# Quantised x of a fused attention and LoRA kernel: transposed by DMA in place of TensorE

## The chip, the cores and the metric

The kernel runs on one core of one Trainium2 chip. The metric is the device time of one execution in microseconds; a comparison uses the median of several runs on the same chip. A core has a TensorE (matrix multiplications, results into PSUM), a VectorE, a ScalarE, a GpSimd ("POOL") and a SyncE ("SP"), each of which runs its own list of instructions in order. SP and ScalarE also issue the DMAs here, each into a queue of its own.

## What is computed

Two steps, for x of shape (2, 1024, 2048):

```python
q1 = fake_quant(layernorm(x), x1_scale, x1_zp)      # 8-bit grid, round and clip
q2 = fake_quant(ctx, x2_scale, x2_zp)
x  = x + q1 @ q2                                    # (1024 x 2048) @ (2048 x 2048) per batch
z  = layernorm(x)
x  = x + z @ kernel + bias + LoRA terms of z        # gated and shared A, B of rank 32
```

The quantised values minus 128 are whole numbers that bf16 holds exactly, so the first product runs in bf16; the second runs in float32.

## The kernel before

Both batches are done one after the other. Tokens are taken in tiles of 128 (`m`, 8 per batch), two tiles make a group `g` (4 per batch), columns of the output go in blocks `n` of 512.

**First product.** ctx arrives in pieces of 128 x 1024 float32 (512 KB) in ten buffers `lit`, loaded by SP ahead of need (`load_next`, L176). `quantise` turns a piece into int16 on ScalarE (L314), into three buffers `q2b`, and into bf16 on VectorE (L317). `prep_x` does the same for a token tile of x: `bn_stats` on VectorE (L283), the mean and root (L257 to L290, with a square root on ScalarE, L261), quantisation to 8 bits on ScalarE (L295), and then, for each half `h` of the 2048 columns, a conversion to bf16 on ScalarE that also sums the row (L298). Both the 8-bit and the bf16 form lie in one work buffer `wk`: `q8` has a place for each of two tiles in turn, `qh` has one place, which each tile overwrites. The product needs x with its 2048 columns on the partitions, so each half of `qh` is transposed: eight 128 x 128 blocks on TensorE against the bf16 identity `ident_h` into the PSUM tile `pt` (L303), and one copy on VectorE from there into `c1T[g]` (L304).

`xattn_pair(b, n, g)` multiplies a group by a column block: per token tile ScalarE writes a correction term into the PSUM tile `pa` (L359), 16 bf16 matmuls of 128 x 512 add to it (L361), and VectorE scales it and adds it to y (L370). `column_term` supplies the correction from ctx (L333, L345, L348).

**Where prep_x stands.** In batch 0: tiles 0 and 1 while the first ctx column block is quantised, tiles 2 and 3 between the first two pairs, tiles 4 to 7 among the later pairs. In batch 1: tiles 0 to 3 inside the last outer step of batch 0's second product (in `meanwhile`), tiles 4 to 7 as in batch 0.

**Second product.** `ffn` multiplies z by the weights with a two-level scheme of seven by seven block products (`product`, L611), with float32 operands that VectorE and POOL combine (L551, L560) and z that is transposed by TensorE (`prep_z`, L432, in float32, against `ident`) and copied by ScalarE (L433). Results are added to y on VectorE (L629) and stored by ScalarE's queue (L631).

**What sets the order.** A scheduling layer places the instructions of each engine, sets the semaphores for every dependence, and gives each DMA of SP and ScalarE one of eight completion semaphores (`DMAHW0` to `DMAHW7`) in turn. A DMA waits until the DMA before it on the same semaphore has landed, whichever queue issued that one. Within an engine and a queue the order is fixed: an instruction that waits holds up everything behind it.

Of the kernel before, what the change touches and what calls it, by code (L numbers as in the profile page):

```python
# [11 lines left out]
BF16 = mybir.dt.bfloat16  # L12
# [8 lines left out]
P = 128  # L21
# [45 lines left out]
def tile_quant_xattn_then_lora_ffn(  # L67
# [17 lines left out]
    nc = tc.nc  # L85
# [12 lines left out]
    H = D // 2  # L98
    KH = KT // 2
# [3 lines left out]
    const = ctx.enter_context(tc.tile_pool(name="const", bufs=1))  # L103
# [4 lines left out]
    ps_m = ctx.enter_context(tc.tile_pool(name="ps_m", bufs=2, space=PSUM))  # L108
# [27 lines left out]
    def bf(t, n):  # L136

        return t.rearrange("p k n -> p (k n)").bitcast(BF16).rearrange("p (k n) -> p k n", n=n)

    def flat(t):  # L140
        return t.rearrange("p k n -> p (k n)")
# [74 lines left out]

    ident = const.tile([P, P], F32, tag="ident", name="ident")
    make_identity(nc, ident)
    ident_h = const.tile([P, P], BF16, tag="ident_h", name="ident_h")
    nc.gpsimd.tensor_copy(ident_h, ident)  # L220
    ones_h = const.tile([P, P], BF16, tag="ones_h", name="ones_h")
    nc.gpsimd.memset(ones_h, 1.0)

# [5 lines left out]
    for tag in ("acc0", "acc1", "delta"):  # L229
# [11 lines left out]
        out=gate_b.rearrange("p b n -> p (b n)"),  # L241
        in_=gate.rearrange("b n -> (b n)").partition_broadcast(P),
# [11 lines left out]
    def norm_stats(stats, name):  # L254

        mv = small.tile([P, 2], F32, tag="mv", name=f"mv_{name}")
        nc.vector.bn_aggr(mv, stats.rearrange("p n s -> p (n s)"))  # L257
        ve = small.tile([P, 1], F32, tag="ve", name=f"ve_{name}")
        nc.vector.tensor_scalar_add(ve, mv[:, 1:2], EPS)
        sd = small.tile([P, 1], F32, tag="sd", name=f"sd_{name}")  # L260
        nc.scalar.activation(sd, ve, AF.Sqrt)  # L261
        r0 = small.tile([P, 1], F32, tag="r0", name=f"r0_{name}")
        nc.vector.reciprocal(r0, sd)

        t = small.tile([P, 1], F32, tag="nt", name=f"nt_{name}")
        nc.vector.scalar_tensor_tensor(t, ve, r0, r0, ALU.mult, ALU.mult)
        nc.vector.tensor_scalar(t, t, -0.5, 1.5, ALU.mult, ALU.add)
        rstd = small.tile([P, 1], F32, tag="rstd", name=f"rstd_{name}")
        nc.vector.tensor_mul(rstd, r0, t)
        return mv[:, 0:1], rstd  # L270
# [6 lines left out]
    def prep_x(b, m, c1T, wk):  # L277

        nm = f"{b}_{m}"
        g, tok = m // MG, ds((m % MG) * P, P)  # L280
        ym = y[g][:, m % MG, :]
        for n in range(NN):
            nc.vector.bn_stats(st1[:, m, n, :], ym[:, ds(n * NB, NB)])  # L283
        mean, rstd = norm_stats(st1[:, m], f"a{nm}")

        k = small.tile([P, 1], F32, tag="kx", name=f"kx_{nm}")
        nc.vector.tensor_mul(k, rstd, inv1)
        o = small.tile([P, 1], F32, tag="ox", name=f"ox_{nm}")
        nc.vector.tensor_mul(o, mean, k)
        nc.vector.tensor_sub(o, z1, o)  # L290

        wf = flat(wk)
        q8 = wf[:, ds((m % 2) * (D // 4), D // 4)].bitcast(U8)
        qh = wf[:, D // 2 : D].bitcast(BF16)
        nc.scalar.activation(q8, ym, AF.Identity, bias=o, scale=k)  # L295
        rsum = small.tile([P, 2], F32, tag="rsum", name=f"rsum_{nm}")
        for h in range(2):
            nc.scalar.activation(  # L298
                qh[:, ds(h * H, H)], q8[:, ds(h * H, H)], AF.Identity, bias=n_centre, accum_out=rsum[:, h : h + 1]
            )  # L300
            pt = ps_m.tile([P, KH, P], BF16, tag="pm", name=f"pt_{nm}_{h}")
            for kt in range(KH):
                nc.tensor.transpose(pt[:, kt, :], qh[:, ds(h * H + kt * P, P)], ident_h)  # L303
            nc.vector.tensor_copy(c1T[g][:, ds(h * KH, KH), tok], pt)  # L304

        r_c = small.tile([P, 1], F32, tag="r_c", name=f"r_c_{nm}")
        nc.vector.tensor_add(r_c, rsum[:, 0:1], rsum[:, 1:2])
        nc.vector.tensor_mul(r_s[:, m : m + 1], r_c, d2)
# [372 lines left out]
    c1T = [bf(t, GT) for t in c1T_bufs]  # L681
# [11 lines left out]
    for b in range(B):  # L693
# [6 lines left out]
        if b == 0:  # L700
            open_c2(0)
            prep_x(0, 0, c1T, wk)
            for r in range(NR):
                quantise(c2[0], r)
                if r == 3:
                    prep_x(0, 1, c1T, wk)
            for m in range(4, MT):
                load_x(0, m)
            open_c2(1)
            column_term(b, 0, c2[0])  # L710
        opened = xattn_pair(b, 0, 0, c1T, c2[0])
        if b == 0:
            for r in range(4):
                quantise(c2[1], r)
            for m in (2, 3):
                prep_x(b, m, c1T, wk)
# [138 lines left out]
        if b + 1 < B:  # L855
            c1T_bufs, c1T, wk = state["c1b"], state["c1T"], state["wk"]
# [53 lines left out]
```

## Time and profile before

| what | value |
|---|---|
| time, median of 3 runs | 1130.41 us (1127.37 to 1130.59) |
| profiled execution, its own time | 1128.61 us |
| its span in the trace | 1126.8 us, granted clock 0.999 |
| TensorE busy | 1072.4 us, 95%, 3926 matmuls |
| VectorE busy | 741.5 us, 66% |
| ScalarE busy | 261.1 us, 23% |
| POOL busy | 266.6 us, 24% |
| SP's DMA queue (q1) | 218.65 MB, 56.6% of 16 engines |
| ScalarE's DMA queue (q10) | 42.02 MB, 10.5% of 16 engines |

The profile page is one execution, recorded by the hardware profiler. Its first part gives each engine's busy time; the second cuts the span into 40 equal slices and gives for each the busy share in tenths; the fourth follows the chain of work that ended last back from the end; the fifth lists groups of instructions by source line (L303 is line 303 of the kernel), with their count, busy time and mean duration, and the idle time of the engine just before them with what ended it. Further views of the trace list the instructions in order of time, the busy time in chosen windows, and the instructions of one tile or one line with their waits. A share of busy time is an average over stages that are limited by different things, so the windows say more than the page's totals.

### The profile page before, as it was taken

Reading aid. Unit: us, or ns where it says so; the run is one execution under the profiler, and the core shown is the slowest. Engines: PE = TensorE matmul, PEld = TensorE weight load, DVE = VectorE, ACT = ScalarE, POOL = GpSimd, SP = SyncE. Lnnn points to the kernel's source line nnn. Section 1 sums busy time; section 2 is a strip of 40 time slices with the busy share of each in tenths; the row PEclk is TensorE's granted clock in tenths of the full one; section 3 lists DMA queues with packets and bytes.
Section 4 is the critical chain, followed back from the end, with each engine's and each line's share of the span. In section 5 each row is a group of like instructions: output and inputs, shape, how many; then the busy total and the mean of one; then the engine's idle time right before and its main releaser. Section 6 shows DMA issues by size and latency. Waiting matters only on the chain.

```text
span 1126.8 us, 10619 instructions
## 1 busy us (share of the span) xinstructions
PE 1072.4 (95%) x3926; PEld 489.3 (43%) x3926; DVE 741.5 (66%) x969; ACT 261.1 (23%) x342; POOL 266.6 (24%) x106
## 2 busy tenths in 40 slices
PE   1689899999999999999999999999999999999998
PEld 0244334554444444444444433455444444444443
DVE  4685547576696768568777654766668586865861
ACT  5875513320001010001375761232000000000000
POOL 0000000234253422525000000022535343243600
PEclk9999999999999999999999999999999999999999
DMA  8991935885789757489857094588668875749611
GB/s 307 391 244 35 282 124 217 298 322 205 246 285 377 266 181 264 141 301 355 285 184 228 1 277 154 182 301 314 244 215 293 295 255 181 256 145 322 213 38 56
DMA packets 120772, 261.35 MB, mean 232 GB/s; under 512 B 11920, under 2 KB 16144, under 8 KB 119568
## 3 DMA queue, kind: packets, MB, share of 16 engines
q1 hardware_dynamic: 99264, 218.65, 56.6%
q10 hardware_dynamic: 21456, 42.02, 10.5%
q8 instruction: 31, 0.51, 0.2%
q14 instruction: 21, 0.17, 0.0%
HBM read 224.99 MB, written 37.75 MB: 233 GB/s over the span
## 4 chain that ended last, share of the span: by engine, by line
PE 80%; DMA 7%; DVE 6%; ACT 4%; issue 1%; SPq 1%; ACTq 0%; DVEq 0%
PE fu L611 33%; PE fv L611 17%; PE pa L361 13%; PE fw L611 9%; DMA lit<-in_ctx_dram 4%; PE pl L483 3%; PE ptz L432 2%; DVE big L560 1%; PE pg_a L383 1%; DVE st L283 1%; PE pg_b L383 1%; ACT big L298 1%; ACT big L295 1%; DMA bd<-q2b 1%; DMA big<-in_w_dram 1%
## 5 line engine op out<-in xcount | busy, mean ns | idle before, releaser
L611 PE MATMUL fu<-big,lit 128*128 128x512 f32 x896 | 396.3, 594 | 2.4 <-DVE y L629 2.4
L560 POOL TENSOR_TENSOR lit<-lit,lit 128x1024 f32<-128x1024 f32 x56 | 165.2, 2957 | 539.4 <-PE pa L361 209.1
L611 PEld LDWEIGHTS fu<-big,lit 128*128 128x128 f32 x896 | 167.8, 190 | 208.2 <-issue 206.7
L361 PE MATMUL pa<-big,big 128*128 128x512 bf16 x1024 | 238.0, 382 | 11.9 <-ACT pa L359 10.6
L611 PE MATMUL fv<-big,lit 128*128 128x512 f32 x448 | 198.1, 594 | 0.0
L551 POOL TENSOR_TENSOR lit<-lit,lit 128x1024 f32<-128x1024 f32 x40 | 100.9, 2524 | 283.4 <-DMA lit<-zs 255.5
L560 DVE TENSOR_TENSOR big<-big,big 128x2048 f32<-128x2048 f32 x56 | 159.4, 2850 | 5.9 <-PE ptz L432 5.3
L361 PEld LDWEIGHTS <-big 128*128 128x128 bf16 x1024 | 97.0, 98 | 146.5 <-issue 44.3
L629 DVE TENSOR_TENSOR y<-y,fu 128x1024 f32<-128x1024 f32 (+1 forms) x98 | 113.7, 1194 | 67.2 <-PE fu L611 66.8
L611 PEld LDWEIGHTS fv<-big,lit 128*128 128x128 f32 x448 | 84.3, 190 | 105.0 <-issue 105.0
L629 DVE TENSOR_TENSOR y<-y,fv 128x1024 f32<-128x1024 f32 x48 | 56.8, 1218 | 91.1 <-PE fv L611 91.1
L478 ACT COPY pl<-bias 128x1024 f32<-128x1024 f32 x32 | 32.6, 1017 | 344.9 <-DVE y L493 327.1
L314 ACT ACTIVATE q2b<-lit,sc,inv 128x1024 int16<-128x1024 f32 x64 | 76.6, 1230 | 146.4 <-DMA lit<-in_ctx_dram 124.7
L551 DVE TENSOR_TENSOR big<-big,big 128x2048 f32<-128x2048 f32 x40 | 101.7, 2544 | 13.2 <-DMA big<-in_w_dram 13.2
L611 PE MATMUL fw<-big,lit 128*128 128x512 f32 x224 | 100.6, 596 | 0.1
L370 DVE SCALAR_TENSOR_TENSOR y<-pa,k_s,y 128x1024 f32<-128x1024 f32 x32 | 41.0, 1282 | 69.7 <-PE pa L361 69.7
L359 ACT ACTIVATE pa<-bp,r_s 128x512 f32<-128x512 f32 x64 | 42.8, 684 | 105.6 <-PE pa L361 60.5
L629 DVE TENSOR_TENSOR y<-y,fw 128x1024 f32<-128x1024 f32 x24 | 28.4, 1217 | 52.5 <-PE fw L611 52.5
L611 PEld LDWEIGHTS fw<-big,lit 128*128 128x128 f32 x224 | 41.3, 190 | 48.7 <-issue 48.2
L303 PE MATMUL pt<-ident_h,big 128*128 128x128 bf16 x256 | 20.3, 231 | 29.6 <-ACT big L298 29.4
L283 DVE BATCH_NORM_STATS2 st<-y 128x6 f32<-128x512 f32 x64 | 42.1, 680 | 2.9 <-DMA y<-in_x_dram 2.9
L317 DVE TENSOR_SCALAR big<-q2b 128x1024 bf16<-128x1024 int16 x64 | 27.6, 440 | 23.7 <-ACT q2b L314 20.5
(79 smaller groups left out, 609.9 us busy)
## 6 DMA issues: line engine op xcount, KB each, us to landing
big<-in_w_dram SPq DMA_DIRECT2D x96, 1024.0 KB
lit<-zs SPq DMA_DIRECT2D x88, 512.0 KB
lit<-in_ctx_dram SPq DMA_DIRECT2D x64, 512.0 KB
out_dram<-y ACTq DMA_DIRECT2D x30, 512.0 KB
zs<-lit ACTq DMA_DIRECT2D x24, 512.0 KB
y<-in_x_dram SPq DMA_DIRECT2D x8, 1024.0 KB
lit<-in_lora_a_dram SPq DMA_DIRECT2D x32, 256.0 KB
lit<-in_lora_bt_dram SPq DMA_DIRECT2D x32, 256.0 KB
```

Source lines behind the costliest of these rows:

```text
L283: nc.vector.bn_stats(st1[:, m, n, :], ym[:, ds(n * NB, NB)])
L314: nc.scalar.activation(qi, t, AF.Relu, bias=z2, scale=inv2)
L317: nc.vector.tensor_scalar(c2[r // 4][:, ds(2 * (r % 4), 2), :], qi, QMAX, CENTRE, ALU.min, ALU.subtract)
L359: nc.scalar.activation(pa[:, j, :], colt[n], AF.Identity, bias=r_s[:, m : m + 1])
L361: nc.tensor.matmul(pa[:, j, :], c1T[g][:, k, ds(j * P, P)], c2[k // 8][:, k % 8, :], start=False, stop=(k == KT - 1), skip_group_check=True,)
L370: summed = nc.vector.scalar_tensor_tensor(yp, pa, s12, yp, ALU.mult, ALU.add)
L478: nc.scalar.copy(pl, self.bb.unsqueeze(1).to_broadcast([P, 2, NB]))
L483: nc.tensor.matmul(pl[:, i, ds(h * (NB // 2), NB // 2)], axT[rows, pr, ds(j * P, P)], self.bp[rows, ds(h * (NB // 2), NB // 2)], start=Fal ...
L551: line(eng.tensor_tensor(got[0], got[0], got[1], ALU.add if terms[1][2] > 0 else ALU.subtract))
L560: line(eng.tensor_tensor(out_t, at[p], at[q], op))
L611: nc.tensor.matmul(ps[:, m, :], at[:, k, ds(m * P, P)], bt[:, k, :], start=(opens and k == 0), stop=(ends and k == KQ - 1), skip_group_che ...
L629: line(nc.vector.tensor_tensor(yp, yp, chains[chain][:, js, :], ALU.add if sign > 0 else ALU.subtract))
```

## The change

In `prep_x`, the eight TensorE transposes of each half and the VectorE copy of their result are replaced by one transposing DMA, issued from ScalarE's queue, which reads the half of `qh` in SBUF and writes it transposed to its place in `c1T[g]`. `ident_h` and the POOL instruction that made it are gone. One half is 128 x 1024 bf16, 256 KB; there are 32 such halves. The PSUM tile `pt` isn't used any more.

```diff
     ident = const.tile([P, P], F32, tag="ident", name="ident")
     make_identity(nc, ident)
-    ident_h = const.tile([P, P], BF16, tag="ident_h", name="ident_h")
-    nc.gpsimd.tensor_copy(ident_h, ident)
     ones_h = const.tile([P, P], BF16, tag="ones_h", name="ones_h")
...
             nc.scalar.activation(
                 qh[:, ds(h * H, H)], q8[:, ds(h * H, H)], AF.Identity, bias=n_centre, accum_out=rsum[:, h : h + 1]
             )
-            pt = ps_m.tile([P, KH, P], BF16, tag="pm", name=f"pt_{nm}_{h}")
-            for kt in range(KH):
-                nc.tensor.transpose(pt[:, kt, :], qh[:, ds(h * H + kt * P, P)], ident_h)
-            nc.vector.tensor_copy(c1T[g][:, ds(h * KH, KH), tok], pt)
+
+            nc.scalar.dma_start_transpose(out=c1T[g][:, ds(h * KH, KH), tok], in_=qh[:, ds(h * H, H)])
```

The scheduling layer places the rest anew: the order of some ScalarE, VectorE and SP instructions around these steps moves by a few places.

## The prediction

> **What bounds the kernel now.** I read the page's slices first, to see which engine is full where, and then the same question in windows around the places where x is prepared. From the page, busy tenths in 40 slices of 28 us:
>
> ```profile
> PE   1689899999999999999999999999999999999998
> ...
> ACT  5875513320001010001375761232000000000000
> ...
> DMA  8991935885789757489857094588668875749611
> ```
>
> TensorE is full from slice 4 on. ScalarE is loaded only in slices 1 to 5 and 20 to 25: the two places where x and ctx of a batch are quantised. All 32 edited steps (16 token tiles, two halves each) lie there, so the rest of the kernel, two stretches of over 300 us of `L611` matmuls, does not change. Then the busy time by window (columns: window, its length, PE, PEld, DVE, ACT, POOL with counts, clock, DMA share, GB/s):
>
> ```profile
> 0.00:30.00 30.00, 4.81 (x22) 2.26 (x22) 13.85 (x51) 16.01 (x17) 1.25 (x10) 1.00 0.82 312
> 30.00:60.00 30.00, 21.79 (x130) 9.85 (x131) 19.84 (x55) 25.51 (x30) 0.00 (x0) 1.00 1.04 373
> 60.00:90.00 30.00, 25.81 (x141) 12.45 (x140) 23.21 (x71) 23.62 (x32) 0.00 (x0) 1.00 0.72 201
> 90.00:120.00 30.00, 29.16 (x172) 13.01 (x171) 18.23 (x37) 15.06 (x18) 0.00 (x0) 1.00 0.33 103
> 560.00:600.00 40.00, 39.16 (x187) 17.55 (x186) 25.76 (x75) 31.21 (x36) 0.00 (x0) 1.00 0.70 232
> 600.00:640.00 40.00, 38.82 (x215) 18.43 (x215) 30.10 (x80) 25.10 (x35) 0.00 (x0) 1.00 0.29 84
> ```
>
> From 30 to 60 us ScalarE is the fullest engine, 25.5 of 30, and the DMA engines are saturated. From 60 us TensorE bounds, with ScalarE at 23.6 of 30 behind it. In batch 1 TensorE has under 1.2 us of slack per 40 us, and ScalarE 8.8 and 14.9. Last the edited step itself, in order of time on ScalarE (start, duration), here tile 2 and the start of tile 3:
>
> ```profile
> 48.51 1.13 ACT L298 ACTIVATE big<-big,n_centre 128x1024 bf16<-128x1024 uint8 x1
> 49.55 0.19 ACT L298 ACTIVATION_READ_ACCUMULATOR big<-big,n_centre 128x1 f32 x1
> 49.64 1.13 ACT L298 ACTIVATE big<-big,n_centre 128x1024 bf16<-128x1024 uint8 x1
> 50.68 0.19 ACT L298 ACTIVATION_READ_ACCUMULATOR big<-big,n_centre 128x1 f32 x1
> 50.77 2.08 ACT L295 ACTIVATE big<-y,ox,kx 128x2048 uint8<-128x2048 f32 x1
> 52.76 0.67 ACT L359 ACTIVATE pa<-bp,r_s 128x512 f32<-128x512 f32 x1
> 53.37 1.13 ACT L298 ACTIVATE big<-big,n_centre 128x1024 bf16<-128x1024 uint8 x1
> ```
>
> ScalarE runs without a gap here: tile 3's `L298` overwrites `qh`, which tile 2's transposes read, only 2.6 us after tile 2's last half was written, and it finds the buffer free. And the transposes, on TensorE and VectorE (count by form, durations, first and last start):
>
> ```profile
> L303 PE MATMUL pt<-ident_h,big x256: 216/219/314, 23.5 to 642.0; 128*128 128x128 bf16 x128
> L304 DVE COPY big<-pt x32: 674/682/692, 24.7 to 643.2; 128x1024 bf16<-128x1024 bf16 x32
> ...
>   ACT big L298: 4.8, 3
> ```
>
> The last line says who waited for them: `L298`, 4.8 us in three places. The profiled run took 1128.6 us for a span of 1126.8, 1.8 under the median of 1130.4; a difference worked out on the trace is added to the median.
>
> [...] 16 transposes in 1.06 us at 52.07 us, 66 ns each, pipelined. [...] an output store that ScalarE issued at 502.02 us behind three loads of SP landed at 510.80, after 8.8 us, between SP's landings at 509.84 and 511.14; the last stores, alone, take 2.7 us.
>
> **What goes.** 256 transposes at 66 ns, 17 us of TensorE. TensorE is waiting anyway at tiles 0 and 1 of batch 0, and mostly at 2 and 3; at the other 12 tiles it is the bound, which makes 12 x 1.06 = 12.7 us the ceiling. 32 copies at 0.682, 21.8 us of VectorE, which is not full anywhere in these windows (at most 30 of 40): worth nothing by themselves. `L298`'s waits for `pt`, 4.8 us, go. I count 6 us of the 12.7, because in these windows TensorE is fed by ScalarE's `L359`, which opens each `pa` and waited for nothing of the removed work except through those 4.8 us: what TensorE saves beyond that it spends waiting for the next `L359`. `ident_h` and its cast (0.29 us on POOL at 1.5 us) go beside the first loads: nothing.
>
> **What comes.** 32 transposing DMAs of 256 KB on ScalarE's own queue, each behind a wait for its half of `L298`. No row of the trace has one, so both ends are bounded.
>
> First, how long ScalarE's queue is held. A plain DMA holds it 0.33 to 0.47 us. [...] I take 1.3[...]: an estimate. Queued behind it are, by the program's order, the `L314` that frees ctx buffers, the `L359` that opens the next `pa`, and the next tile's `L295`/`L298`. 32 x 1.3 = 41.6 us of ScalarE. In 20 to 60 us, four tiles put 10.4 us where 30 to 60 has 4.5 idle: 6 on the path. In 60 to 112, 10.4 us meet 6.4 idle to 90 and more after: 2 on the path. Batch 1 puts 20.8 on 56.3 busy of 80, 77 of 80, while half of those gaps are waits for VectorE's statistics (`L261`, `L295`) that do not move: 5 on the path. Sum 13.
>
> Second, when the data lands. [...] the round trip of an idle store is 2.7 us, so about 3 us alone. In 20 to 60 us SP keeps a queue: the ctx load issued at 21.25 landed at 34.3, 13 us later. A transpose among these takes between 4 and 10 us. New in the program is that the next tile's `L298` waits for this landing, because `qh` is one buffer. Tiles 0 and 1 have four ctx quantisations between them and hide it. Tile 3 follows tile 2 with one: I count 5 us of stall on ScalarE there, with everything queued behind. At tiles 5 and 7 and in batch 1 the DMA share is 0.3 to 0.7, and about 3 us lie under `L295` (2.08) and `L359` (0.67). Sum 5, from 0 to 15.
>
> Third, semaphores. DMAs take eight completion semaphores in turn, and a DMA waits until the previous one on its semaphore has landed. In the program tile 2's second half waits for a ctx load of SP, tile 3's two halves for two more, tile 4's and 5's for lora_a loads; in the trace these landed at 37 to 43 and by 63 us, before the transposes stand there (54 and 85 us): nothing, unless the loads slip. The other way, SP's second round of ctx loads (issued from 21.25 us) now waits for tile 0's second transpose, some 8 to 12 us later. The cover is the 13 us of loads in flight; if the transpose lands later, the DMA engines run dry, up to 3 us. SP's order otherwise differs by a few lora and b_sh loads: nothing. POOL's has only the cast less.
>
> **Sum:** -6 + 13 + 5 = +12 us: span 1138.8, profiled run 1140.6, on the median **1142**.
>
> **Rivals.** (a) *Not slower:* [...] Place: the same windows. [...] if the landing is 3 us as well, only the -6 stays: 1125. For it: plain DMAs hold ScalarE 0.4 us. Against it: [...] the DMA queue of the first 60 us. It decides below about 0.7 us of hold with landings under 4 us; between, up to about 0.9, the terms cancel and the time is within 0.3% (3.4 us, about what a measurement of this kernel can tell from no change): 1130.
> (b) *Much slower:* transposes do not stream[...]. Then `L298` of almost every second tile, and in batch 1 of each, waits for the landing: [...] about 1190 and more. [...]
> That the transposes would not happen is excluded: the built program has 32 of them on ScalarE and no `L303`.
>
> **How the numbers follow.** My case (1134 to 1160) has 0.57[...]. (a) has 0.17 and the cancelling terms 0.10. (b) has 0.16, a third of it below 1172. The range runs from 1122, a little below (a), to 1172, which leaves out about 0.05 below and 0.11 above. Faster 0.17, same 0.10, slower 0.73.
>
> **What will show it.** Right: DMA issues of over 1 us on ScalarE's queue at the transposing line; idle of ScalarE before `L298` ended by a DMA, longest at tile 3; the first `pa` pair of the second ctx block (67.5 us before) about 10 us late, part of it won back by 112 us, the rest kept through `L611`; TensorE's busy time about 17 us less and its idle time some 29 more. Wrong: issues of half a microsecond with no idle before `L298` (then a), landings over 8 us outside the first 60 us (then b), or a stall at a transpose itself behind an SP load, which I priced at nothing.

## The result and the profile after

The changed kernel takes 1139.51 us (median of 4 runs, 1138.43 to 1144.99) beside 1128.95 for the kernel before (4 runs, one more than ahead of the prediction): ratio 1.0103, 95% interval 1.0066 to 1.0141. It is slower. The profiled execution took 1138.43 us for a span of 1136.6, against 1128.61 and 1126.8 before: +9.8 us.

In the kernel after, line numbers move: the transposing DMA is L300, `L298` is now L296, `L295` L293, `L314` L310, `L359` L355, `L361` L357, `L370` L366 and `L611` L607. From the page of the kernel after, the busy tenths in 40 slices:

```profile
PE   1369999999999999999998899999999999999998
...
ACT  3657612321000000000266861232100000000000
...
DMA  8998855886779847579989584588668875648611
```

TensorE's second and third slices (28 to 85 us) read 3 and 6 where they read 6 and 8: most of the loss is there. Slices 22 and 23, where batch 1 is prepared, read 8 and 8 for 9 and 9. The windows of the kernel after (columns as in the prediction):

```profile
30.00:60.00 30.00, 13.15 (x38) 3.71 (x39) 13.15 (x46) 21.00 (x22) 0.00 (x0) 1.00 0.95 304
60.00:90.00 30.00, 19.61 (x80) 7.52 (x80) 20.52 (x61) 18.50 (x24) 0.00 (x0) 0.94 0.97 241
90.00:120.00 30.00, 28.95 (x132) 12.31 (x133) 12.50 (x27) 19.80 (x29) 0.00 (x0) 1.00 0.70 155
...
600.00:640.00 40.00, 33.07 (x150) 13.53 (x152) 25.74 (x69) 28.71 (x35) 0.00 (x0) 1.00 0.87 248
```

From 30 to 60 us TensorE does 13.2 us of work instead of 21.8, and ScalarE, the fullest engine before with 25.5 of 30, only 21.0: it too is kept from working. Two words are used from here on: a DMA's hold is the time for which its issue occupies the queue of the issuing engine, and its landing is the arrival of its data, counted from the start of the issue. The order of time on ScalarE at tile 0 shows by what (start, duration; ACTq is ScalarE's queue of instructions that issue DMAs):

```profile
23.44 1.34 ACTq L300 DMA_TRANSPOSE big<-big  x1
24.36 0.19 ACT L296 ACTIVATION_READ_ACCUMULATOR big<-big,n_centre 128x1 f32 x1
24.82 5.66 ACTq L300 DMA_TRANSPOSE big<-big  x1
30.53 1.24 ACT L310 ACTIVATE q2b<-lit,sc,inv 128x1024 int16<-128x1024 f32 x1 [5.99 <-issue]
```

The first transposing DMA holds the queue for 1.34 us, the second for 5.66, and the next ctx quantisation, before which ScalarE is idle for 6.0 us, stands behind it. Tile 1 does the same with 1.60 and 4.50. The waits of the kernel after between 20 and 80 us (who waited for whom: us in total, times, longest) carry this on to TensorE:

```profile
PE pcp L329 <- DVE big L313: 25.2, 7, 8.9
DVE big L313 <- ACT q2b L310: 14.5, 6, 6.9
ACT q2b L310 <- issue: 13.1, 3, 6.0
```

The three lines are read from the bottom up: `L310` stands behind the issues for 13.1 us, VectorE's clipping (L313) waits for `L310`, and TensorE's column sums (L329), which must be done before the first `pa`, wait for VectorE. (TensorE waited 27.5 us in this window before, too, for `L298` at its transposes; what is new is the 13.1.) The view of the transposing line itself (min/median/max in ns, first and last start; then who waited for it to land):

```profile
L300 ACTq DMA_TRANSPOSE big<-big x32: 1247/1258/5661, 23.4 to 654.0; - x32
...
  PEld L357: 10.7, 5
  PE pa L357: 8.7, 4
  ACT big L296: 0.6, 1
```

An undisturbed issue holds ScalarE for 1.25 us; all 32 together hold it for 55.3, of which 20.4 fall on the first four tiles. `L296`, which was to wait for `qh`, waits 0.6 us in the whole run; TensorE waits 8.7 for landings.

As one measure across all runs I use when VectorE reads each finished `pa` pair (`L370` before). The table gives in us how much later than in the kernel before that is. Its head names pairs by their time before: the first two and the eleventh of batch 0, and one early and the last of batch 1. "Worst" is the largest value in batch 0. These values are of the profiled execution, the ratio is of all runs; in e10 and e11 the profiled execution was 4.2 and 3.7 us slower than the median:

| kernel | 52.3 | 64.7 | worst | 148.5 | 615.8 | 749.2 | ratio (95%) |
|---|---|---|---|---|---|---|---|
| after | 10.7 | 15.3 | 19.4 | 10.6 | 14.2 | 9.9 | 1.0103 (1.0066-1.0141) |
| e1_te_first4 | 0.2 | 0.2 | 4.6 | 0.1 | 1.5 | -2.9 | 0.9991 (0.9981-1.0000) |
| e2_dma_first4 | 10.2 | 16.8 | 19.6 | 16.5 | 17.7 | 18.1 | 1.0172 (1.0157-1.0186) |
| e3_sp_queue | -0.1 | 20.9 | 20.9 | 3.7 | 10.7 | 6.6 | 1.0069 (1.0057-1.0081) |
| e5_dma_late | -0.1 | -0.1 | 5.3 | 0.9 | 2.0 | 0.1 | 0.9998 (0.9988-1.0008) |
| e9_dma_b1_01 | 0.2 | 0.2 | 0.2 | -0.7 | -0.3 | 2.2 | 1.0020 (1.0010-1.0029) |
| e10_half | 3.8 | 13.9 | 17.5 | 13.2 | 18.8 | 22.2 | 1.0161 (1.0143-1.0179) |
| e11_plain_copy | 3.9 | 21.8 | 26.2 | 17.5 | 30.1 | 24.6 | 1.0194 (1.0170-1.0218) |
| e12_ahead4 | 14.8 | 18.8 | 24.5 | 15.3 | 17.9 | 13.7 | 1.0130 (1.0113-1.0146) |
| e13_half_qh2 | -0.3 | 8.0 | 12.6 | 7.6 | 13.7 | 12.1 | 1.0116 (1.0102-1.0131) |
| e14_split_after | 13.6 | 25.8 | 38.4 | 29.7 | 41.0 | 35.7 | 1.0330 (1.0311-1.0349) |
| e15_split_before | -4.2 | 0.2 | 1.4 | -0.6 | 4.4 | 4.4 | 1.0015 (1.0005-1.0025) |
| e18_few_loads | 7.1 | 17.6 | 21.4 | 13.9 | 16.6 | 12.5 | 1.0141 (1.0118-1.0164) |

The changed kernel is 19.4 us late at its worst, wins 8.8 of that back by 148 us, and is still 9.9 late at the last pair.

### The profile page after: what moved, and what is told of

Its sections match the earlier page's. It is cut to its first block, busy times and chain, and to the rows that moved or that the text cites. A ratio compares the mean times of both kernels' runs of the same rounds, so it can differ in the third digit from the quotient of the medians.

```text
span 1136.6 us, 10077 instructions
## 1 busy us (share of the span) xinstructions
PE 1059.4 (93%) x3641; PEld 474.6 (42%) x3670; DVE 736.1 (65%) x937; ACT 261.5 (23%) x342; POOL 267.0 (23%) x105
## 3 DMA queue, kind: packets, MB, share of 16 engines
q10 hardware_dynamic: 55248, 50.41, 15.1%
## 5 line engine op out<-in xcount | busy, mean ns | idle before, releaser
L607 PE MATMUL fu<-big,lit 128*128 128x512 f32 x896 | 395.7, 594 | 2.4 <-DVE y L625 2.4
L607 PEld LDWEIGHTS fu<-big,lit 128*128 128x128 f32 x896 | 168.0, 190 | 209.4 <-issue 208.2
L357 PE MATMUL pa<-big,big 128*128 128x512 bf16 x995 | 233.9, 384 | 16.9 <-DMA big<-big 8.7
L607 PE MATMUL fv<-big,lit 128*128 128x512 f32 x448 | 197.7, 594 | 0.0
L556 DVE TENSOR_TENSOR big<-big,big 128x2048 f32<-128x2048 f32 x56 | 165.4, 2956 | 5.9 <-PE ptz L428 5.3
L357 PEld LDWEIGHTS <-big 128*128 128x128 bf16 x1024 | 97.8, 99 | 156.6 <-issue 43.3
L607 PEld LDWEIGHTS fv<-big,lit 128*128 128x128 f32 x448 | 84.5, 190 | 106.0 <-issue 106.0
L310 ACT ACTIVATE q2b<-lit,sc,inv 128x1024 int16<-128x1024 f32 x64 | 76.6, 1231 | 158.1 <-DMA lit<-in_ctx_dram 126.1
L547 DVE TENSOR_TENSOR big<-big,big 128x2048 f32<-128x2048 f32 x40 | 104.9, 2621 | 10.9 <-DMA big<-in_w_dram 10.9
L607 PE MATMUL fw<-big,lit 128*128 128x512 f32 x224 | 100.6, 596 | 0.0
L366 DVE SCALAR_TENSOR_TENSOR y<-pa,k_s,y 128x1024 f32<-128x1024 f32 x32 | 41.1, 1284 | 71.8 <-PE pa L357 71.6
L355 ACT ACTIVATE pa<-bp,r_s 128x512 f32<-128x512 f32 x64 | 42.9, 682 | 101.4 <-PE pa L357 50.7
L607 PEld LDWEIGHTS fw<-big,lit 128*128 128x128 f32 x224 | 41.3, 190 | 48.6 <-issue 48.2
L329 PE MATMUL pcp<-big,ones_h 128*32 128x512 bf16 x128 | 15.7, 419 | 40.8 <-DVE big L313 40.7
L313 DVE TENSOR_SCALAR big<-q2b 128x1024 bf16<-128x1024 int16 x64 | 27.4, 439 | 31.8 <-ACT q2b L310 27.2
```

The lines of the kernel that those rows point to most:

```text
L310: nc.scalar.activation(qi, t, AF.Relu, bias=z2, scale=inv2)
L313: nc.vector.tensor_scalar(c2[r // 4][:, ds(2 * (r % 4), 2), :], qi, QMAX, CENTRE, ALU.min, ALU.subtract)
L355: nc.scalar.activation(pa[:, j, :], colt[n], AF.Identity, bias=r_s[:, m : m + 1])
L357: nc.tensor.matmul(pa[:, j, :], c1T[g][:, k, ds(j * P, P)], c2[k // 8][:, k % 8, :], start=False, stop=(k == KT - 1), skip_group_check=True,)
L366: summed = nc.vector.scalar_tensor_tensor(yp, pa, s12, yp, ALU.mult, ALU.add)
L547: line(eng.tensor_tensor(got[0], got[0], got[1], ALU.add if terms[1][2] > 0 else ALU.subtract))
```

## The experiments

### Where the loss sits: e1, e2, e5, e9

My theory after the result was A: the loss is ScalarE's hold at the first tiles, long because SP has a backlog of loads there. Rival B: each transposing DMA costs its share, wherever it stands. In e1, tiles 0 to 3 of batch 0 keep the TensorE transposes:

```diff
+            if not (b == 0 and m < 4):
+                nc.scalar.dma_start_transpose(out=c1T[g][:, ds(h * KH, KH), tok], in_=qh[:, ds(h * H, H)])
+                continue
             pt = ps_m.tile([P, KH, P], BF16, tag="pm", name=f"pt_{nm}_{h}")
```

> Tiles 0 to 3 of batch 0 go back to TensorE transposes with a VectorE copy; the other 12 tiles stay on DMA. Theory A (ScalarE held at the issue of the first transposes, 13.1 us before the first pa matmul, by a DMA backlog that only the first 70 us have): the whole loss of 10.3 us sits in these four tiles, so the first pa matmul is back at 42 to 43 us and the time is that of before or a little less, 1124 to 1131 (TensorE sheds 12 us of transposes in the other tiles, and batch 1 as a whole gained 0.5 in the changed kernel). Theory B (the cost is one of each transposing DMA, a landing of 3 us or more that TensorE or the buffer qh waits for, in every tile): three quarters of the loss stay, 1136 to 1138.

1127.65 beside 1128.64. The whole loss is gone. e2 is the opposite cut, `if b == 0 and m < 4`:

> The opposite cut: only tiles 0 to 3 of batch 0 go by DMA, the other 12 tiles by TensorE. Theory A: the first pa matmul at 52 to 53 us as in the changed kernel, and the whole loss, 1137 to 1142. Theory B: a quarter of the loss, 1131 to 1133.

1147.88: the whole loss, and 6 us above the upper end of what I expected. B has fallen with these two: the cost belongs to four tiles of sixteen. The surplus says what the other 12 tiles are worth. The difference of the ratios of e2 and of the changed kernel, 0.0069, is 7.8 us (with the two intervals about 3 to 12), which those tiles win when batch 0 is already late. In e1 the same 12 tiles win 1.0. In e1's waits of TensorE up to 125 us one sees where it goes:

```profile
PE pa L364 <- ACT pa L362: 8.8, 8, 2.2
PE pa L364 <- DMA big<-big: 4.1, 1, 4.1
```

The first line is little more than before (7.6). The four tiles of batch 0 that e1 moves spare TensorE 64 x 66 ns = 4.2 us, and it waits 4.1 for the landing of one of them. Two further cuts ask whether any part is worth keeping: e5 (`if m >= 4`, both batches) and e9 (`if b == 1 and m < 2`).

> DMA only for the tiles 4 to 7 of each batch (16 of 32 halves), where ScalarE waited for no issue and no load backlog stands; TensorE for tiles 0 to 3 of both batches. Theory A: nothing is lost at the start, and 64 x 2 transposes of TensorE (8.5 us) are shed, of which at most half counts: 1122 to 1130. Theory B: half of the loss stays, 1133 to 1136.

> Only tiles 0 and 1 of batch 1, whose transposes lay in TensorE's queue inside the end of the first ffn, go by DMA; all others by TensorE. In the run with the first four tiles on TensorE the first pa pair of batch 1 was 6 us earlier than before, and this was lost again at tiles 2 and 3. If that loss is ScalarE's hold at those tiles: 1122 to 1126, about 4 us faster than before. If ScalarE has no room for an earlier start anyway (TensorE then waits for the quantised ctx): 1127 to 1129, no change.

1128.35 and 1129.71 beside 1128.64 and 1127.71: no gain, and in e9 a loss of 0.2%, just above both of its forecasts. Away from the first four tiles the change is worth next to nothing: what TensorE sheds in batch 0 turns into one wait for a landing (4.1 us in e1, 5.5 in e5). e1 is the best version found, within 0.3% of the kernel before.

### Is it ScalarE's hold? e3, e10, e11

e3 issues all 32 from SP's queue (`nc.sync.dma_start_transpose`), so that ScalarE isn't held at all. Rival C: the late ctx loads of SP are the cost.

> All 32 transposing DMAs are issued from SP's queue, none from ScalarE's. Theory A: ScalarE is not held any more, so its chain of quantisations is as in the kernel before; SP is held instead, and while it waits for qh its ctx loads wait behind: first pa matmul 43 to 48 us, time 1127 to 1135. Theory C (the semaphores and the late ctx loads are what costs, SP's second round of ctx loads having been 13.4 us late in the changed kernel, not ScalarE's hold): SP's loads get still later, first pa matmul at 52 us or more, 1139 to 1150.

1136.52, between the two. The first pair is on time, though SP's ctx loads are late here as well (the one of 19.82 us goes out at 31.50): so the 10.7 us there were ScalarE's hold, and C falls for this pair. But the second pair is 20.9 late: the hold has moved with the DMA, for SP's queue is now held 23.7 us by the first eight (62.1 by all), and tile 2's transposes, issued at 56.27 and 61.38, land at 68.2 and 70.6. Not all of the 20.9 is waiting: the scheduling layer placed this pair behind the next one here and tile 3's quantisation at 76.85; in the order in which the pairs are read the largest lag is 10.5. e10 takes the long holds away in another manner, with only one transposing DMA per tile (`if h == 0`; the second half by TensorE):

> In all 16 tiles only the first half of x goes by DMA, the second half by TensorE, so that no transposing DMA is issued directly behind another. Theory A1 (the long holds of 4.5 and 5.7 us come from the second DMA finding the first one's descriptors still in ScalarE's queue): every hold is 1.25 to 1.6 us, about 20 us in all instead of the changed kernel's 55, the first pa matmul is at 44 to 46 us, time 1126 to 1132. Theory A2 (the hold is long because the DMA engines are busy with SP's loads, whichever DMA it is): the first halves of tiles 0 and 1 are held for 4 us or more, the first pa matmul is at 48 to 52, time 1132 to 1137.

The holds are as A1 said, 1.25 to 1.55 us, 20.8 in all. The time is not: 1146.99, slower than with 55 us of hold. In order of time on ScalarE in e10 (L302 the DMA, L298 the quantisation of x, L317 of ctx):

```profile
53.60 1.38 ACTq L302 DMA_TRANSPOSE big<-big  x1
...
55.75 1.23 ACT L317 ACTIVATE q2b<-lit,sc,inv 128x1024 int16<-128x1024 f32 x1
66.44 1.15 ACT L298 ACTIVATE big<-big,n_centre 128x1024 bf16<-128x1024 uint8 x1 [9.46 <-DMA big<-big]
```

Tile 2's transpose is issued at 53.6, 7 us earlier than in the changed kernel, and meets SP's x loads of tiles 4 to 7. It lands 12.8 us later, and tile 3 waits for `qh` meanwhile, 9.5 us; tile 1 waited 4.1. TensorE waits for landings as well, 11.7 us. So the long hold can't be the whole cause: theory A falls in this form. e11 goes further and replaces the transposing DMA by a plain copy of the same bytes in nearly as many packets (2080 for a pair where a pair of transposes has 2112), into the same place. It leaves the transposition out:

```diff
-            nc.scalar.dma_start_transpose(out=c1T[g][:, ds(h * KH, KH), tok], in_=qh[:, ds(h * H, H)])
+            nc.scalar.dma_start(
+                out=c1T[g][:, ds(h * KH, KH), tok],
+                in_=qh[:, ds(h * H, H)].rearrange("p (k q) -> p k q", q=P),
+            )
```

> The changed kernel with a plain DMA copy of the same 256 KB from qh to the same place, in rows of 256 bytes (1024 of them, where the transposing DMA counts 1056 packets): it leaves the transposition out, and keeps every wait, queue and semaphore. Theory P1 (the number of descriptors fills the queue, whatever they do): holds as long as with the transposing DMA, first pa matmul at 50 to 53, 1136 to 1142. Theory P2 (making the transposing descriptors costs the time on ScalarE's queue): holds of about 0.4 us, no long second hold, first pa matmul at 42 to 45, 1124 to 1131.

1149.74. The view of the copying line in e11 (L360 the product, L296 the quantisation of x):

```profile
L300 ACTq DMA_DIRECT2D big<-big x32: 601/602/765, 23.4 to 668.5; - x32
...
  PE pa L360: 22.4, 3
  ACT big L296: 18.5, 5
```

Holds of 0.60 us and never a long one, even for the second of a pair: the number of packets alone doesn't make the long hold (P1's holds fall). That only a pair of transposes does isn't shown: in e11 two output stores issued right behind a pair of copies were held 2.71 and 2.25 us, and in e3 the first transposes of tiles 0 and 2 were held 2.77 and 5.01 us behind SP's plain loads. Yet the time is no better than e10's, so P2's time falls too. The copies land after 10.4, 10.0, 13.2, 12.6, 15.1 and 14.9 us at tiles 0 to 2, and the price is paid as waits for `qh` (18.5 us) and of TensorE (22.4).

### The latency behind SP's loads: e13, e12, e18

That made theory D: DMAs of both queues share the engines and complete nearly in the order of issue, so in the first 75 us a transpose lands only after the loads that SP had issued before it. This latency would be the cost, paid by whichever comes first: ScalarE at the next issue, ScalarE at `qh`, or TensorE at the product. e13 is e10 with a second bf16 `qh` for the odd tiles of batch 0 (the expectation calls it int8):

```diff
+    qx = lit.take()
...
-        qh = wf[:, D // 2 : D].bitcast(BF16)
+        qh = (flat(qx) if b == 0 and m % 2 else wf[:, D // 2 : D]).bitcast(BF16)
```

> The kernel with only the first halves by DMA (1147, 18 us slower than before, though its holds were 1.25 to 1.55 us), with a second buffer for the int8 values of odd tiles in batch 0, taken from the ten load buffers, so that tiles 1 and 3 do not wait until the transposes of tiles 0 and 2 have landed (4.1 and 9.5 us on ScalarE). If that wait for qh is where the latency was paid: no idle of ScalarE ended by a DMA at that line, 1132 to 1138. If TensorE then waits for the same landings: 1142 to 1147, with its waits for transposes above 12 us.

1142.48, 4.5 us better than e10 and just inside the second forecast. ScalarE's waits for `qh` fall from 16.1 to 2.8 us, the first pair is on time, and TensorE waits instead, once, for the landing of tile 2's transpose (issued 49.42, landed 62.08). That is 9.8 us, less than the 12 I had forecast. From the view of e13's transposing line:

```profile
  PE pa L365: 9.8, 1
  ACT big L299: 2.8, 1
```

ScalarE pays a part again, too. With the wait for `qh` gone, tile 3's transpose is issued while tile 2's is in flight, and a long hold appears in a kernel with one transpose per tile:

```profile
52.83 5.60 ACTq L303 DMA_TRANSPOSE big<-lit  x1
```

e12 was to shorten the backlog by issuing fewer ctx loads ahead (`ahead[0] = 9` to 4):

> The changed kernel with 4 instead of 9 ctx loads issued ahead of use, so that the transposing DMAs of tiles 0 and 1 meet a shorter backlog of SP. If the length of the second hold is set by when the first transpose lands behind that backlog: first landing 5 to 7 us instead of 10.3, second hold 2 to 3.5 us instead of 5.7. If the second hold is a price of the instruction: 5.7 as before. The time is not settled by this, since the ctx loads come later as well: 1135 to 1145.

1142.72. The first landing is 10.26 us and the second hold 5.34: hardly changed, because the backlog hardly was. With a free buffer and no other wait SP went on to the x loads of tiles 2 and 3 and to further ctx loads; the one issued last before the transpose landed at 31.73, the transpose at 33.59. At tile 1 the x loads of tiles 4 to 7 now stood in front: landing 11.43 instead of 8.70, second hold 7.19 instead of 4.50. So this run doesn't test what it was made for, but its tile 1 agrees with D. e18 takes the buffers themselves away until tile 3 is done, and moves the x loads behind the tiles before them:

```diff
+    held = [lit.take() for _ in range(5)]
     ahead[0] = 9
     load_next()
-    load_x(0, 2)
-    load_x(0, 3)
...
                     prep_x(0, 1, c1T, wk)
-            for m in range(4, MT):
-                load_x(0, m)
+                    load_x(0, 2)
+                    load_x(0, 3)
...
                 prep_x(b, m, c1T, wk)
+            for t in held:
+                lit.give(t)
+            for m in range(4, MT):
+                load_x(0, m)
```

> The changed kernel with 5 of the 10 load buffers kept back until tile 3 of batch 0 is quantised, and the x loads of tiles 2 to 7 placed after the tiles before them, so that SP can't run ahead: at tile 0's transposes it has one ctx load and one x load outstanding (about 4 us of DMA) instead of six loads (11 us). Theory D (the landing is SP's backlog at the issue, and the second hold follows the first landing): first landing 5 to 7.5 us instead of 10.3, second hold 1.3 to 3.5 us instead of 5.7, likewise at tile 1 (8.7 and 4.5 in the changed kernel), first pa matmul at 44 to 49; the time 1130 to 1138, if the ctx loads keep up. Theory F (the backlog doesn't matter; a transposing DMA among loads takes 8 to 12 us whatever stands before it, as with the loads cut in two): landing 8 us or more, hold 4 or more, 1139 or above.

1144.31. In order of time on ScalarE in e18, tiles 0 and 2:

```profile
23.35 1.54 ACTq L299 DMA_TRANSPOSE big<-big  x1
...
24.93 4.64 ACTq L299 DMA_TRANSPOSE big<-big  x1
...
58.46 7.00 ACTq L299 DMA_TRANSPOSE big<-big  x1
```

Where the backlog is shorter the landing follows: at tile 0 7.37 us instead of 10.28, at tile 1 5.58 instead of 8.70, and the first pair is 7.1 late instead of 10.7. The hold fell less than I expected at tile 0 (4.64), and as expected at tile 1 (3.17). But the x loads of tiles 4 to 7 have only moved in front of tile 2, whose transpose lands after 11.77 us with a hold of 7.00, and all that was won is lost there. D is right on these landings, and my forecast of the time was wrong. The place in the order, for seven transposes of four kernels:

| transpose | landing of the last load that SP had issued before it | its own landing |
|---|---|---|
| after, tile 0 | 33.19 | 33.72 |
| e12, tile 0 | 31.73 | 33.59 |
| e12, tile 1 | 49.75 | 50.45 |
| e18, tile 0 | 29.66 | 30.71 |
| e10, tile 2 | 64.61 | 66.41 |
| after, tile 3 | 70.84 | 74.75 |
| e18, tile 2 | 65.24 | 68.65 |

The first five follow within 2 us. The last two don't, and before e18's tile 2 two ctx loads landed that SP issued after it (66.75 and 68.29): the order of issue is not quite it. The packets in the trace say more. In the changed kernel from 28 to 31 us, with tile 0's transposes under way (q1 is SP's queue, q10 ScalarE's; packets, MB, share of 16 engines):

```profile
q1 hardware_dynamic: 225, 0.95, 95.3%
q10 hardware_dynamic: 225, 0.06, 8.5%
```

The queues took turns packet by packet, 225 for 225, but a packet of SP had 4.2 KB on average and one of the transposes 0.25. From 32 to 34 us, when SP's loads were nearly out, 1642 packets of the transposes passed and 31 of SP. It is the same with e10's tile 2 (554 and 586 from 57 to 63 us) and with the plain copies of e11 (158 and 157 from 28 to 30). So D's latency is that of a thousand small packets which take turns with large ones: most pass only when SP's backlog is nearly through, whichever was issued first. For the first 3.5 us after its issue no packet of tile 0's transpose passed at all (1.1 in idle engines at 634.24); why is open.

A rival is that the transposes only take time of full DMA engines, so that loads and then ScalarE are late. SP's loads are late, but in the changed kernel ScalarE waits for none of them between 20 and 80 us.

### A run that D does not explain: e14, with its control e15

Both cut every ctx and x load into smaller DMAs; e14 is the changed kernel so, e15 the kernel before.

```diff
-        return [ctx_in[b, ds(2 * r * P, 2 * P), ds(n * NB, NB)].rearrange("(k p) n -> p k n", p=P)]
+        return [ctx_in[b, ds((2 * r + c) * P, P), ds(n * NB, NB)] for c in range(2)]
...
-        nc.sync.dma_start(out=y[m // MG][:, m % MG, cols], in_=x[b, ds(m * P, P), cols])
+        for q in range(cols.start // NB, cols.stop // NB):
+            nc.sync.dma_start(out=y[m // MG][:, m % MG, ds(q * NB, NB)], in_=x[b, ds(m * P, P), ds(q * NB, NB)])
```

> The changed kernel with every ctx load (1 MB) cut in 2 DMAs and every x load in pieces of 512 columns, the same bytes in the same order. With eight completion semaphores at most eight DMAs are in flight, so half the size means half the backlog that a transposing DMA of ScalarE stands behind. Theory D (DMAs of all queues complete nearly in the order of issue, so a transpose issued in the first 70 us lands only after all loads of SP that were issued before it; that latency is the loss, and it is paid as ScalarE's hold, as a wait for qh or as a wait of TensorE, whichever comes first): the first transpose lands after 5 to 7 us instead of 10.3, the second hold is 1.3 to 3 us instead of 5.7, and the time is 1128 to 1134, at most 5 above the kernel before with the same cut. Theory E (the loss is a price of each transpose or of the queue's own length, not of SP's backlog): landing 10 us, hold 5.7, 1137 to 1141, 10 above.

> The control of the cut loads: the kernel before with the same smaller load DMAs and no transposing DMA. The DMA engines keep their work, SP issues twice the DMAs: within 3 us of the kernel before, 1127 to 1131.

(A ctx load is 512 KB, cut into two of 256, not the 1 MB of the expectation.) The control is 1130.43, as expected. e14 is 1164.87. The loads in flight at tile 0's first transpose were all landed 3.6 us after its issue, and still it landed after 7.9 us and the second after 11.7: neither D nor E. Nor do the packets take turns one for one: from 22 to 26 us 1037 of the transposes pass and 260 of SP. SP's waits in e14 from 20 to 100 us, and a window of it:

```profile
SPq L179 <- DMA big<-big: 18.3, 5, 5.1
SPq L187 <- DMA big<-big: 11.8, 2, 7.5
```

```profile
20.00:30.00 10.00, 2.44 (x8) 0.42 (x8) 2.93 (x13) 6.83 (x8) 0.00 (x0) 1.00 1.15 205
```

SP stands 30 us at semaphores that a transpose holds, and the DMA engines, with a share of 1.15, move 205 GB/s, where e15 moved 383 in the same window. So the transposes delay SP as well in this kernel, both at the shared semaphores and on the engines; here it made x late (VectorE waited 14.5 us for it). Which of the two weighs more no run separates.

## Why the prediction was right, step by step

The total was right: 1142 for 1139.5, slower by 10.6 us where it had 12. Its terms were less so, and that they add up is in part luck: the loss came from long second holds and late landings in a quarter of the tiles, which the prediction had priced lower there, while batch 1, where it had 5, lost nothing in the end.

**What goes, -6.** Measured against e2, the 12 tiles won 7.8 us (about 3 to 12); 6 was near. But the term isn't a constant: e1 shows 1.0 for the same tiles when nothing is late. The gain existed because the loss did.

**First hold, +13.** The price of 1.3 us was an estimate of mine that no trace of the kernel before could show; it came out at 1.25. Its sum wasn't right: 55.3 us of hold instead of 41.6, and 20.4 instead of 10.4 in the first four tiles. Its places were wrong as well. I had 8 us in batch 0 and 5 in batch 1; batch 0 lost 10.6 (at the 148.5 us pair) and batch 1 as a whole nothing (9.9 at the end). Between, the pairs went from 7.3 to 14.6 us late and back; the transposes that TensorE sheds in batch 1 (128 x 66 ns, 8.4 us) lie against the holds there, and no run of mine separates the two.

**Second, landing, +5.** The durations were right: 7.9 to 10.3 us at tiles 0 and 1, where I had 4 to 10, and 3.1 where nothing else runs, where I had about 3. The step that failed is "Tile 3 follows tile 2 with one: I count 5 us of stall on ScalarE there". `L296` waited 0.6 us. The latency came at the issue of the second half, 5.66 and 4.50 us at tiles 0 and 1, which I had priced at nothing, and as 8.7 us of waits of TensorE. The stall that I had described is real, though: e10, in which the second halves' issues are gone, has it with 9.5 us at tile 3. In the changed kernel the long holds had already delayed tile 2's transposes to 60.5 us, when SP, stopped by the semaphores (9.3 us behind a transpose between 38 and 62 us), had less in flight: its queue took 57.6% of 16 engines from 60.5 to 65.4 us, for 95.3% from 28 to 31. They landed after 4.9.

**Third, semaphores, 0.** SP's reload went from 21.25 to 34.66 us, 13.4 later where I had 8 to 12, and the DMA engines moved 304 GB/s instead of 373 from 30 to 60 us. ScalarE waited for no ctx load there: nothing, as predicted. e14 shows that this cover is thin.

**What would show it.** The issues of over 1 us were there. The second ctx block's first pair was 18 us late (read by VectorE at 94.8 for 76.7; its matmuls began at 85.1 for 67.5), not 10, and of this some 8 us were won back. TensorE's busy time fell by 13.0 (17 expected), and its idle time rose by 22.8 (29); both are upper ends, since the trace after lacks 29 of the 1024 `pa` matmuls, up to 6.7 us by an estimate from the 238.0 us of all of them before. The idle of ScalarE before `L298`, which should have been longest at tile 3, did not appear. The stall at a transpose itself, which the prediction named as a sign against it, appeared. One reading was off: the store at 502.02 us, which landed between two of SP's loads, stood behind five loads of SP in flight, not three.

**The rivals.** The prices of a transpose from which the rivals' times and the upper end of my range follow weren't shown by any trace of the kernel before. (a) fell on its price: an undisturbed issue takes 1.25 us, and (a) needed less than about 0.7. e11 adds that a short hold alone, 0.60 us, would not have made it true: with landings of 10 to 15 us it is 1.9% slower. Its condition of landings under 4 us mattered as much. (b), in which transposes do not stream, fell on the idle landing of 3.1 us; after the first 60 us no landing took more than 7.7.

## What to carry to other kernels

Before a step is moved from an engine to a DMA, look at what is in flight on the DMA engines at that moment. Here the move traded 1.06 us of TensorE per tile for landings of 7.9 to 10.3 us among SP's loads (tiles 0 and 1) and of 3.1 with nothing else in flight. Removing the visible wait only showed the next one: in e10 the long holds were gone and ScalarE waited 16.1 us for `qh`, in e13 2.8 and TensorE 9.8. What helped was to leave those four tiles alone (1127.65 us in e1). And what TensorE shed counted where it was late: the same 12 tiles won 7.8 us (about 3 to 12) when batch 0 was late and 1.0 in e1.

## What the runs showed of the hardware that I had not expected

- A second transposing DMA, issued while the first was in flight among loads, was held for 2.2 to 5.7 us in the first four tiles of the changed kernel, and was let go 1.1 to 3.7 us before the first landed (tile 0: 30.48 and 33.72). At batch 1's tile 0, where SP's queue took only 19.1% of 16 engines (577 to 580 us), the hold was 1.28, let go 0.7 before. There is no fixed distance: in e14's tile 1 it was 5.8 us. A plain copy of the same size and nearly the same packets was never held beyond 0.77 us. Why is open.
- The transposing rate. ScalarE's DMA queue took 15.1% of 16 engines instead of 10.5%, 53 us of all engines for 32 transposes: 1.7 us each. The first eight were issued from 23.4 to 68.5 us, and in the kernel before the DMA share from 20 to 60 us was 1.04 already. Alone, between 634 and 639 us, a pair ran at about 213 GB/s. It isn't the transposition that makes it slow: the plain copies of e11 in 256-byte rows, alone between 644 and 646 us, ran at about 218.
- TensorE's granted clock was low in places where it had been 1.00 before. In the changed kernel it was 0.50 from 74.8 to 78.0 us, which costs at most 1.6 us by an estimate (half of the 3.2); in e10 it was 0.75 on average from 60 to 80 us, in e14 0.63 from 80 to 100, at most 5.0 and 7.4 us by the same estimate (the missing share of 20 us). e15, with no transposing DMA, had 0.50 from 20 to 40 us with hardly a loss (ratio 1.0015). Part of the losses of the changed kernel and of e10 to e18 may be this; no run separates it.
